# A one-hot cut into six pieces and two adds cut into halves, one such operation per unit, in a graph layer on one core

## The chip, the core and the metric

The kernel runs on one core of a Trainium2 chip. A core has five engines that run side by side and wait for each other by semaphores: TensorE (matmuls, into PSUM), VectorE, ScalarE, GpSimd and SyncE, which issues DMAs. In the profile they are called PE, DVE, ACT, POOL and SP; PEld is TensorE's loading of weights. In this kernel the DMAs that gather rows by index are issued from GpSimd, the plain ones from SyncE and, at the start and the end, ScalarE.

The metric is the device time of one execution in microseconds, lower is better. It is given as a median over several runs. The profile shows one execution.

## The reference

The layer works on 6250 nodes with 256 features and 206,250 edges (100,000 in both directions and a loop per node), sorted by destination. Cut to what matters:

```
h = relu(layernorm(x))                                   # without weights
e = relu(raw @ W_e1.T + b_e1) @ W_e2.T + b_e2            # per edge, 64 -> 256 -> 256
edge_emb = (e * (polarity + 0.01)) @ W_le.T + b_le
msg  = relu(h[src] + edge_emb)                           # a row of h gathered per edge
aggr = segment_sum(msg, dst)                             # 33 edges per node on average
t    = relu(layernorm((h + aggr) @ W_g1.T + b_g1) * ln_g + ln_b)
out  = x + t @ W_g2.T + b_g2
```

All of it is fp32.

## The kernel before

**Edges.** A tile is 128 edges, a block four tiles (512 edges), a group six blocks (3072 edges). There are 403 blocks and 68 groups, the last group of one block. Half a block, 256 edges, is called a unit; there are 806. W_e2 and W_le are multiplied into one 256x256 matrix first. The main loop runs over units u. For each it calls, in this order:

- `forward(u)`: `edge_part(u)` makes four matmuls of the unit into one PSUM buffer (line 266), of which the pool has seven, and VectorE adds a bias row and writes the result to SBUF (line 271). When u mod 4 is 1, and in the body of the run only when u mod 8 is 1, `turn_of` follows: the first layer of two pairs of blocks (line 243, 16 matmul records, eight PSUM buffers), its relu into SBUF by ScalarE (line 251) and in part VectorE (line 248), then `add_pairs`, the segment sums of finished blocks. This is called a turn below.
- `gathers(...)`: GpSimd issues the gathers of rows h[src], two per unit (line 528), tied to the last matmul of the unit. A buffer `hg` takes the rows of one unit, and there are 16.
- `whole(v)`, for a unit v that lies 22 units back at the start and one unit back at the end of the run: VectorE multiplies the edge part by the polarity, a column scalar of the tile, and adds the gathered rows (line 551, two products per unit), and ScalarE takes the relu (line 556). In the iteration of u mod 8 equal to 0 none is made in the body of the run, in the next one two.
- `due()`: one operation from a list of things that have come due. In units 0 and 1 of each eight it takes none.

**Segment sums.** `add_up` (line 566) sums a tile's messages by a matmul whose weights are a one-hot, 128 edges by 32 rows of the tile's window, one for each tile. `select(g)` makes the one-hots of a whole group in one VectorE instruction: it compares a row of 32 numbers with the rows of edges `rel`, 128 x 768 elements (line 541). It is put on the list two units after the first block of group g - 2 has been summed; three such buffers exist.

**Nodes.** The 49 windows of 128 nodes are finished as their last group is summed. `node_work(w)` puts its steps on the same list: `spread` loads x, x transposed (`hT`) and the row statistics and makes the one-hots of the window (line 629); three and four units later `ready(0)` and `ready(1)` multiply and add the statistics to `hT` (line 639, 128 x 256 each); five units later `offset` adds the last bias to x (line 205, 128 x 256). Then come `rows_of` (lines 664 and 666: sums per node, and h + aggr), `one`, `two`, `three` (the two matmuls, the layer norm, and the output).

VectorE takes its instructions in the order in which the program issues them. So in each unit its queue holds: the add of line 271, in a turn the relu of line 248, the products, and what the list gave. Line numbers are those of the kernel before.

Of the kernel before, what the change touches and what calls it, by code (L numbers as in the profile page):

```python
# [17 lines left out]
P = 128  # L18
# [33 lines left out]
def group_of(b):  # L52
    return b // L
# [40 lines left out]
def gnn_kernel(ctx: ExitStack, tc: tile.TileContext, x, src_c, dst_c, dst_r, pol_c, raw_t, w_e1t, w_e2,  # L94
# [16 lines left out]

    ident = const.tile([P, P], F32, name="ident")
    eps_t = const.tile([P, 1], F32, name="eps_t")
    we1_s = const.tile([P, D], F32, name="we1_s")
    wc_s = const.tile([P, 2, D], F32, name="wc_s")
    bc_s = const.tile([P, 2, D], F32, name="bc_s")
# [27 lines left out]
    def finish_nodes(nd, ps, w, n):  # L144

        r = w * P

        def turn(a):
            pt = ps()
            for c in range(2):  # L150
                nc.tensor.transpose(pt[:, 0, c * P:c * P + n], a[:n, c * P:(c + 1) * P], ident[:n, :n])
            aT = nd.tile([P, 2, P], F32, name="aT")
            if n == P:
                nc.scalar.activation(aT, pt[:, 0, :].rearrange("p (c n) -> p c n", c=2), AF.Copy)
            else:
                for c in range(2):
                    nc.scalar.activation(aT[:, c, :n], pt[:, 0, c * P:c * P + n], AF.Copy)
            return aT

        def first(aT, bias_by_pe=False):  # L160
            ph = ps()
            if bias_by_pe:
                nc.tensor.matmul(ph[:n, 0, :], ones[0:1, :n], bg1_b[0:1], start=True, stop=False)
            for c in range(2):
                nc.tensor.matmul(ph[:n, 0, :], aT[:, c, :n], wg1_s[:, c, :], start=c == 0 and not bias_by_pe, stop=c == 1)  # L165
            hs = nd.tile([P, D], F32, name="hs")
            if bias_by_pe:
                hb = ph[:, 0, :]
            else:
                hb = hs  # L170
                nc.vector.tensor_add(hs[:n], ph[:n, 0, :], bg1_b[:n])
            mv = row_stats(nd, n, 1, lambda i: hb[:n])
            rs = nd.tile([P, 1], F32, name="rs1")
            one_over_std(rs[:n], mv, n)
            nc.vector.tensor_scalar(hs[:n], hb[:n], mv[:n, 0, 0:1], rs[:n], op0=ALU.subtract, op1=ALU.mult)
            return hs

        def second(hs):
            pt = ps()
            for c in range(2):  # L180
                nc.tensor.transpose(pt[:, 0, c * P:c * P + n], hs[:n, c * P:(c + 1) * P], ident[:n, :n])  # L181
            nT = nd.tile([P, 2, P], F32, name="nT")
            for c in range(2):
                nc.scalar.activation(nT[:, c, :n], pt[:, 0, c * P:c * P + n], AF.Relu, bias=lnb_s[:, c:c + 1],  # L184
                                     scale=lng_s[:, c:c + 1])
            return nT

        def third(nT, xt):
            po = ps()
            for c in range(2):  # L190
                nc.tensor.matmul(po[:n, 0, :], nT[:, c, :n], wg2_s[:, c, :], start=c == 0, stop=c == 1)  # L191
            ot = nd.tile([P, D], F32, name="ot")
            nc.vector.tensor_add(ot[:n], po[:n, 0, :], xt[:n])
            for i, (a, b) in enumerate(spread_out(n)):
                eng = nc.scalar if i else nc.sync
                eng.dma_start(out=out[bass.ds(r + a, b - a), :], in_=ot[a:b])

        def load_x():
            xt = nd.tile([P, D], F32, name="xt3")
            for a, b in spread_out(n):  # L200
                nc.sync.dma_start(out=xt[a:b], in_=x[bass.ds(r + a, b - a), :])
            return xt

        def offset(xt):
            nc.vector.tensor_add(xt[:n], xt[:n], bg2_b[:n])

        return turn, first, second, third, load_x, offset

# [3 lines left out]
    with fast:  # L212
# [87 lines left out]
                turn_of(u // 4)  # L300

        nc.vector.memset(eps_t, EPS)
        nc.vector.memset(ones, 1.0)
        nc.vector.memset(rs_s, 0.0)
        nc.vector.memset(nm_s, 0.0)
# [207 lines left out]
        with tc.tile_pool(name="hg", bufs=HG) as hg_p, tc.tile_pool(name="ms", bufs=5) as ms_p, \  # L513
# [21 lines left out]

            def select(g):

                n = len(blocks_of(g)) * S
                t = g * L * S
                sel[g] = sel_p.tile([P, L * S, W], F32, name="sel")  # L540
                nc.vector.tensor_tensor(  # L541
                    sel[g][:, :n, :], iota_w.rearrange("p (o w) -> p o w", o=1).to_broadcast([P, n, W]),
                    rel[:, t:t + n].rearrange("p (t o) -> p t o", o=1).to_broadcast([P, n, W]), ALU.is_equal)

            def whole(u):

# [11 lines left out]
            def add_up(b):  # L558

                g = group_of(b)  # L560
                k = b - g * L
                if k == 0:
                    acc[g] = pd[:, g % 2, :] if g < NG - 1 else ps()[:, 0, :]
                for j in range(S):
                    m = hg[2 * b + j // 2]
                    nc.tensor.matmul(acc[g][j * W:(j + 1) * W, :], sel[g][:, k * S + j, :], m[:, j % 2, :],  # L566
                                     start=k == 0, stop=b == blocks_of(g)[-1])
                hg.pop(2 * b)
                hg.pop(2 * b + 1)
                return g if b == blocks_of(g)[-1] else None  # L570
# [16 lines left out]
            def add_pairs(last=False):  # L587

                nonlocal summed
                whole_groups = []  # L590
                while summed < NP and min(4 * summed + 4, NU) < made + last:
                    for b in (2 * summed, 2 * summed + 1):
                        if b < NB:
                            whole_groups.append(add_up(b))
                            if b % L == 0 and group_of(b) + 2 < NG:
                                at(now + 2, lambda g=group_of(b) + 2: select(g))
                    summed += 1

                for g in whole_groups:
                    keep(g)  # L600
# [2 lines left out]
            todo = {}  # L603
            now = 0
            late = {}
            ending = {-2: [], -1: []}

            def at(u, fn):
# [2 lines left out]
            def node_work(w, spread_now=False):  # L611
# [7 lines left out]
                def spread():  # L619
                    box["xt"] = load_x()  # L620
                    box["hT"] = nd.tile([P, 2, P], F32, name="hT")
                    nc.sync.dma_start(out=box["hT"][:, :, :n], in_=x_t[:, :, w * P:w * P + n])
                    st = nd.tile([P, 2, P], F32, name="stb")
                    nc.sync.dma_start(out=st, in_=st_d[w:w + 1].to_broadcast([P, 2, P]))
                    box["st"] = st
                    box["sel2"] = []
                    for g in gs:
                        s2 = sel2_p.tile([P, P], F32, name="s2")
                        nc.vector.tensor_scalar(s2, iota_p, rowid[:, g:g + 1], float(-w * P), op0=ALU.subtract,
                                                op1=ALU.is_equal)  # L630
                        box["sel2"].append(s2)
                    at(now + 3, lambda: ready(0))
                    at(now + 4, lambda: ready(1))
                    at(now + 5, lambda: offset(box["xt"]))

                def ready(i):

                    hT, st = box["hT"], box["st"]
                    nc.vector.tensor_tensor(hT[:, :, :n], hT[:, :, :n], st[:, i:i + 1, :n].to_broadcast([P, 2, n]),  # L639
                                            (ALU.mult, ALU.add)[i])  # L640

                def sums_of(part):

# [56 lines left out]

            gathers(HG)
            sums = add_pairs
            for i, fn in ((0, first_rows), (1, rows_of_edges), (3, lambda: select(0)), (5, row_numbers), (6, stats_out),
                          (7, lambda: select(1)), (8, node_weights)):
                at(LEAD + i, fn)
            for i, fn in enumerate((by_group(0, ALU.max), by_group(1, ALU.min), by_row(0, ALU.max), by_row(1, ALU.min),
                                    verdict, count, total)):
# [2 lines left out]
            for u in range(LEAD, NU):  # L710
# [8 lines left out]
                else:  # L719
                    gathers(4 * summed + HG - 4 + (u - TURN) % 4 + 1, last_z)  # L720

                while made < u + 1 - max(LEAST, LEAD - u // SHRINK) - (by_two(u // 4) and (u + 1) % 8 == TURN):
                    whole(made)
                    made += 1
                due()
                if u == NU - 24:
                    for w in range(NW):
                        if groups_of(w)[-1] == NG - 1:
                            late[w] = node_work(w, True)
                if u == LEAD + 60:  # L730
                    flag = nc.values_load(bad_i[0:1, 0:1], min_val=0, max_val=3 * P)
            while todo:
                now = min(todo)
                for fn in todo.pop(now):
                    fn()
            before, last = ending[-2], ending[-1]
            for sums_of, halves_out, rows_of, one, two, three, gs in before:
                rows_of()
# [28 lines left out]
def any_order(tc, dram, v):  # L767
# [7 lines left out]
    with tc.tile_pool(name="sc", bufs=1) as sc, tc.tile_pool(name="sk", bufs=2) as sk, \  # L775
# [78 lines left out]
        def nodes(w, n):  # L854
# [1 line left out]
            nc.sync.dma_start(out=ac[:n], in_=acc_d[bass.ds(w * P, n), :])  # L856
            turn, one, two, three, load_x, offset = v["finish_nodes"](sk, lambda: sp1.tile([P, 1, D], F32, name="ps_a"), w, n)
            xt = load_x()
            offset(xt)
            three(two(one(turn(ac))), xt)  # L860

        with tc.For_i(0, full, 1) as w:
# [65 lines left out]
```

## Time and profile before

| | |
|---|---|
| median of 3 runs | 2187.48 us (2186.34 to 2188.13) |
| profiled execution | 2189.23 us, its span 2187.4 us |
| mean granted TensorE clock | 0.997 |
| busy: TensorE, VectorE, ScalarE, GpSimd | 2169.5, 1604.4, 960.8, 1648.4 us |
| gathers, line 528 | 1612, 999 ns each in the mean |
| products, line 551 | 1612, 478 ns |
| add of the edge part, line 271 | 799, 685 ns |
| one-hot, line 541 | 68, 940 ns |
| add and multiply of h, line 639; of x, line 205 | 98, 417 ns; 49, 416 ns |

The span runs from the first to the last instruction of the program. "Busy" is time in which an engine executed an instruction, not time in which it did so at its best. A row of the groups names line, engine, operation, out<-in and shapes, then the count, the busy time, the mean length of one, and the idle time of the engine ahead of these instructions with what ended it. A row of the waits gives the total, the number of times and the longest. A row of the timeline gives the start, the length, and how many instructions were merged into it.

### The profile page before, as it was taken

Reading aid. Unit: us, or ns where it says so; the run is one execution under the profiler, and the core shown is the slowest. Engines: PE = TensorE matmul, PEld = TensorE weight load, DVE = VectorE, ACT = ScalarE, POOL = GpSimd, SP = SyncE. Lnnn points to the kernel's source line nnn. Section 1 sums busy time; section 2 is a strip of 40 time slices with the busy share of each in tenths; the row PEclk is TensorE's granted clock in tenths of the full one; section 3 lists DMA queues with packets and bytes.
Section 4 is the critical chain, followed back from the end, with each engine's and each line's share of the span. In section 5 each row is a group of like instructions: output and inputs, shape, how many; then the busy total and the mean of one; then the engine's idle time right before and its main releaser. Section 6 shows DMA issues by size and latency. Waiting matters only on the chain.

```text
span 2187.4 us, 34907 instructions
## 1 busy us (share of the span) xinstructions
PE 2169.5 (99%) x12382; PEld 1625.1 (74%) x12382; DVE 1604.4 (73%) x3470; ACT 960.8 (44%) x1701; POOL 1648.4 (75%) x1675
## 2 busy tenths in 40 slices
PE   9999999999999999999999999999999999999998
PEld 6677777777777777777677777777777777777776
DVE  7787777777777777777677777777777767777675
ACT  7444444444444444444444444343444444444443
POOL 5777777777777777777777777777777777777775
PEclk9999999999999999999999999999999999999999
DMA  9544445454545454545544445445444445454543
GB/s 313 159 134 134 138 126 157 130 149 122 151 126 155 119 155 125 151 123 151 142 122 139 142 139 151 129 121 156 139 131 128 143 130 153 131 146 130 150 123 89
DMA packets 156075, 309.17 MB, mean 141 GB/s; under 512 B 33183, under 2 KB 77944, under 8 KB 155896
## 3 DMA queue, kind: packets, MB, share of 16 engines
q0 software_dynamic: 77376, 211.39, 33.7%
q1 hardware_dynamic: 77364, 92.23, 13.7%
q10 hardware_dynamic: 1156, 3.28, 0.4%
q8 instruction: 98, 1.61, 0.3%
q14 instruction: 81, 0.66, 0.1%
HBM read 293.92 MB, written 12.85 MB: 140 GB/s over the span
## 4 chain that ended last, share of the span: by engine, by line
PE 92%; DMA 3%; POOL 2%; DVE 2%; issue 1%; ACT 1%; ACTq 0%; DVEq 0%; POOLq 0%
PE pz L266 60%; PE pz L243 16%; PE pd L566 9%; PE pz L664 3%; DMA hg<-hb_d,src_s 3%; PE pz L165 2%; PE pz L191 2%; POOL hg L528 2%; DVE msg L271 1%; PE pz L181 1%; DMA xt<-in_x_dram 0%; ACT xt L366 0%; DVE hg L551 0%; DVE st L136 0%; PE pz L307 0%
## 5 line engine op out<-in xcount | busy, mean ns | idle before, releaser
L528 POOL DMA_INDIRECT hg<-hb_d,src_s x1612 | 1611.2, 999 | 495.5 <-issue 355.3
L266 PE MATMUL pz<-wc_s,e 128*128 128x256 f32 x6448 | 1452.3, 381 | 1.3 <-ACT msg L269 1.3
L266 PEld LDWEIGHTS pz<-wc_s,e 128*128 128x128 f32 x6448 | 1208.7, 190 | 203.8 <-issue 28.8
L556 ACT ACTIVATE hg<-hg 128x512 f32<-128x512 f32 x805 | 500.5, 629 | 1048.0 <-DVE hg L551 1030.5
L551 DVE SCALAR_TENSOR_TENSOR hg<-msg,pol_s,hg 128x256 f32<-128x256 f32 x1612 | 711.3, 478 | 153.3 <-DMA hg<-hb_d,src_s 148.9
L271 DVE TENSOR_TENSOR msg<-pz,bc_s 128x512 f32<-128x512 f32 x799 | 542.9, 685 | 224.0 <-PE pz L266 223.0
L243 PE MATMUL pz<-raw,we_s 64*128 64x512 f32 x1612 | 402.8, 608 | 6.9 <-DVE msg L271 6.6
L251 ACT ACTIVATE e<-pz,vecs 128x512 f32<-128x512 f32 x605 | 361.8, 692 | 88.0 <-PE pz L243 86.9
L243 PEld LDWEIGHTS pz<-raw,we_s 64*128 64x128 f32 x1612 | 160.2, 186 | 195.6 <-issue 127.2
L248 DVE TENSOR_SCALAR e<-pz,vecs 128x512 f32<-128x512 f32 x201 | 150.5, 749 | 164.6 <-PE pz L243 164.6
L566 PE MATMUL pd<-hg,sel 128*32 128x256 f32 x3216 | 196.9, 386 | 0.0
L566 PEld LDWEIGHTS pd<-hg,sel 128*32 128x32 f32 x3216 | 95.0, 110 | 129.3 <-issue 77.6
L664 PEld LDWEIGHTS pz<-s,ms 128*128 128x128 f32 x548 | 68.7, 192 | 3.1 <-issue 0.4
L664 PE MATMUL pz<-s,ms 128*128 128x128 f32 x548 | 69.3, 275 | 0.1
L541 DVE TENSOR_TENSOR sel<-iota_w,rel 128x768 f32<-128x768 f32 x68 | 63.9, 940 | 0.0
L370 POOL TENSOR_TENSOR hb<-xt,rows_b 128x256 f32<-128x256 f32 (+1 forms) x49 | 34.1, 728 | 24.2 <-ACT xt L366 18.2
L191 PE MATMUL pz<-wg_s,nT 128*128 128x256 f32 (+1 forms) x196 | 50.6, 380 | 0.6 <-ACT nT L184 0.6
L165 PE MATMUL pz<-wg_s,hT 128*128 128x256 f32 (+1 forms) x196 | 50.5, 380 | 0.0
L577 ACT ACTIVATE ms<-pd 128x256 f32<-128x256 f32 x66 | 25.4, 384 | 51.5 <-PE pd L566 51.5
L191 PEld LDWEIGHTS pz<-wg_s,nT 128*128 128x128 f32 (+1 forms) x196 | 37.1, 190 | 5.9 <-ACT nT L184 0.8
L165 PEld LDWEIGHTS pz<-wg_s,hT 128*128 128x128 f32 (+1 forms) x196 | 37.0, 190 | 5.7 <-issue 0.3
L639 DVE TENSOR_TENSOR hT<-hT,stb 128x256 f32<-128x256 f32 x98 | 40.8, 417 | 0.0
(90 smaller groups left out, 378.2 us busy)
## 6 DMA issues: line engine op xcount, KB each, us to landing
raw<-in_raw_t_dram SPq DMA_DIRECT2D x202, 256.0 KB
hg<-hb_d,src_s POOLq DMA_INDIRECT x1612
stb<-st_d SPq DMA_DIRECT2D x49, 128.0 KB
hb_d<-hb SPq DMA_DIRECT2D x12, 512.0 KB
xt<-in_x_dram SPq DMA_DIRECT2D x48, 128.0 KB
hT<-in_x_t_dram SPq DMA_DIRECT2D x48, 128.0 KB
out_dram<-ot SPq DMA_DIRECT2D x48, 128.0 KB
xt<-in_x_dram SPq DMA_DIRECT2D x11, 512.0 KB
```

The costliest lines, as they stand in the source:

```text
L165: nc.tensor.matmul(ph[:n, 0, :], aT[:, c, :n], wg1_s[:, c, :], start=c == 0 and not bias_by_pe, stop=c == 1)
L191: nc.tensor.matmul(po[:n, 0, :], nT[:, c, :n], wg2_s[:, c, :], start=c == 0, stop=c == 1)
L243: nc.tensor.matmul(pe[s, c], we1_s[s * F:(s + 1) * F, c * P:(c + 1) * P], raw[q][s * F:(s + 1) * F, :], start=True, stop=True)
L248: nc.vector.tensor_scalar(e1[b][:, c, :], pe[s, c], be1_s[:, c:c + 1], 0.0, op0=ALU.add, op1=ALU.max)
L251: nc.scalar.activation(e1[b][:, c, :], pe[s, c], AF.Relu, bias=be1_s[:, c:c + 1])
L266: last_z = nc.tensor.matmul(pz[:, i, :], e1[b][:, c, k:k + P], wc_s[:, c, :], start=c == 0, stop=c == 1)
L271: nc.vector.tensor_add(msg[u], pz, bc_s)
L528: g = nc.gpsimd.indirect_dma_start(out=hg[u][:, i, :], out_offset=None, in_=hb_d, in_offset=bass.IndirectOffsetOnAxis(ap=src_s[:, 2 * u + ...
L551: nc.vector.scalar_tensor_tensor(hg[u][:, i, :], m[:, i, :], pol_s[:, 2 * u + i:2 * u + i + 1], hg[u][:, i, :], op0=ALU.mult, op1=ALU.add)
L556: nc.scalar.activation(hg[u], hg[u], AF.Relu)
L566: nc.tensor.matmul(acc[g][j * W:(j + 1) * W, :], sel[g][:, k * S + j, :], m[:, j % 2, :], start=k == 0, stop=b == blocks_of(g)[-1])
L664: nc.tensor.matmul(pa[:, c, :n], ms[g][:, c * P:(c + 1) * P], box["sel2"][i][:, :n], start=i == 0, stop=i == len(gs) - 1)
```

## The change

`select` no longer issues its instruction. It returns one entry per block of the group, and these are put into a queue `rest`; each entry makes the one-hots of one block's four tiles, 128 x 128 elements. `ready` and `offset` work on one half of 128 columns per call, and their four and two calls are put into a queue `steps`, due three units after `spread`. In each unit `piece()` takes one entry: from `steps` if its first is due, else from `rest`. It is called behind `forward` and `gathers` and ahead of `whole`. When more than six entries are in `rest`, a second one is taken behind `due`. `add_up` takes out what is still left for its group.

All three operations become a `scalar_tensor_tensor` whose scalar is a column of zeros, `zero_c`: (tensor + 0) op tensor. They were `tensor_tensor`. The values computed are the same.

```diff
+    zero_c = const.tile([P, 1], F32, name="zero_c")
...
-        def offset(xt):
-            nc.vector.tensor_add(xt[:n], xt[:n], bg2_b[:n])
+        def offset(xt, c):
+            h = slice(c * P, (c + 1) * P)
+            nc.vector.scalar_tensor_tensor(xt[:n, h], xt[:n, h], zero_c[:n], bg2_b[:n, h], op0=ALU.add, op1=ALU.add)
...
+        nc.vector.memset(zero_c, 0.0)
...
             def select(g):
-                n = len(blocks_of(g)) * S
-                t = g * L * S
-                sel[g] = sel_p.tile([P, L * S, W], F32, name="sel")
-                nc.vector.tensor_tensor(
-                    sel[g][:, :n, :], iota_w.rearrange("p (o w) -> p o w", o=1).to_broadcast([P, n, W]),
-                    rel[:, t:t + n].rearrange("p (t o) -> p t o", o=1).to_broadcast([P, n, W]), ALU.is_equal)
+                return [(g, lambda k=k: rows_of_block(g, k)) for k in range(len(blocks_of(g)))]
+
+            def rows_of_block(g, k):
+                t = (g * L + k) * S
+                if k == 0:
+                    sel[g] = sel_p.tile([P, L * S, W], F32, name="sel")
+                nc.vector.scalar_tensor_tensor(
+                    sel[g][:, k * S:(k + 1) * S, :], iota_w.rearrange("p (o w) -> p o w", o=1).to_broadcast([P, S, W]),
+                    zero_c, rel[:, t:t + S].rearrange("p (t o) -> p t o", o=1).to_broadcast([P, S, W]), op0=ALU.add,
+                    op1=ALU.is_equal)
+
+            def piece():
+                if steps and steps[0][0] <= now:
+                    steps.popleft()[1]()
+                elif rest:
+                    rest.popleft()[1]()
...
                 if k == 0:
                     acc[g] = pd[:, g % 2, :] if g < NG - 1 else ps()[:, 0, :]
+                    while rest and rest[0][0] <= g:
+                        rest.popleft()[1]()
...
                             if b % L == 0 and group_of(b) + 2 < NG:
-                                at(now + 2, lambda g=group_of(b) + 2: select(g))
+                                rest.extend(select(group_of(b) + 2))
...
-                    at(now + 3, lambda: ready(0))
-                    at(now + 4, lambda: ready(1))
-                    at(now + 5, lambda: offset(box["xt"]))
+                    steps.extend((now + 3, lambda i=i, c=c: ready(i, c)) for i in range(2) for c in range(2))
+                    steps.extend((now + 3, lambda c=c: offset(box["xt"], c)) for c in range(2))

-                def ready(i):
+                def ready(i, c):
                     hT, st = box["hT"], box["st"]
-                    nc.vector.tensor_tensor(hT[:, :, :n], hT[:, :, :n], st[:, i:i + 1, :n].to_broadcast([P, 2, n]),
-                                            (ALU.mult, ALU.add)[i])
+                    nc.vector.scalar_tensor_tensor(hT[:, c, :n], hT[:, c, :n], zero_c, st[:, i, :n], op0=ALU.add,
+                                                   op1=(ALU.mult, ALU.add)[i])
...
-            for i, fn in (..., (3, lambda: select(0)), ..., (7, lambda: select(1)), (8, node_weights)):
+            for i, fn in (..., (3, lambda: rest.extend(select(0) + select(1))), ..., (8, node_weights)):
                 at(LEAD + i, fn)
...
+                piece()
                 while made < u + 1 - max(LEAST, LEAD - u // SHRINK) - (by_two(u // 4) and (u + 1) % 8 == TURN):
                     whole(made)
                     made += 1
                 due()
+                if len(rest) > 6:
+                    piece()
...
+            while steps:
+                steps.popleft()[1]()
```

The path `any_order`, taken only for inputs in another order, calls `offset` for both halves; it isn't run here.

## The prediction

> **What bounds the kernel now.** I read the head of the page first, then the groups by line, then the waits, and last the timeline around single gathers. By the head TensorE is busy for 99% of the span and GpSimd for 75%:
>
> ```profile
> span 2187.4 us, 34907 instructions
> PE 2169.5 (99%) x12382; PEld 1625.1 (74%) x12382; DVE 1604.4 (73%) x3470; ACT 960.8 (44%) x1701; POOL 1648.4 (75%) x1675
> ```
>
> That 75% misleads. The gathers of line 528 have these rows in the groups, in the view of their line (shortest/median/longest, first and last start) and in the waits (total, times, longest):
>
> ```profile
> L528 POOL DMA_INDIRECT hg<-hb_d,src_s x1612 | 1611.2, 999 | 495.5 <-issue 355.3
> ...
> L528 POOL DMA_INDIRECT hg<-hb_d,src_s x1612: 940/947/2088, 64.5 to 2168.0; - x180
> ...
> POOL hg L528 <- PE pz L266: 39.6, 130, 0.3
> POOL hg L528 <- ACT hg L556: 26.5, 87, 0.3
> ```
>
> The reader is to see that busy and idle add up: 1611.2 + 495.5 is, but for 2.3 ahead of the first, the whole stretch from 64.5 us to the end of the last at 2168.9, and the idle is 495.5 / 1612 = 0.31 us ahead of each gather, no longer after a wait for TensorE or ScalarE than without one. GpSimd goes from gather to gather without being starved once. Its time is 1612 x (0.947 + 0.305) = 2018 us plus what the gathers take over their median, 1612 x (999 - 947) = 84 us.
>
> TensorE pays for the lateness in the first layer's turns:
>
> ```profile
> L243 PE MATMUL pz<-raw,we_s 64*128 64x512 f32 x1612 | 402.8, 608 | 6.9 <-DVE msg L271 6.6
> ...
> 1190.54 3.70 PE L243 MATMUL pz<-raw,we_s 64*128 64x512 f32 x16
> ...
> 1014.55 4.83 PE L243 MATMUL pz<-raw,we_s 64*128 64x512 f32 x16
> ...
> 1017.40 0.29 PEld L243 LDWEIGHTS pz<-raw,we_s 64*128 64x128 f32 x2 [0.84 <-DVE msg L271]
> ...
> DVE hg L551 <- DMA hg<-hb_d,src_s: 148.9, 199, 2.8
> ```
>
> A clean turn takes 3.70 us for 16 records, the one at 1014.55 takes 4.83 because a PSUM buffer still waits for VectorE's add. VectorE is late since its products wait for gathered rows (148.9 us). Over all turns 402.8 - 1612/16 x 3.70 = 30 us are lost, with the 6.9 idle 37 us. TensorE could thus end at about 2187.4 - 37 = 2150, GpSimd without its excess 84 us earlier than now. GpSimd is the bound, and TensorE stands 37 us behind it.
>
> **Where the 84 us come from.** The timeline puts it on VectorE instructions with two SBUF tensors:
>
> ```profile
> 1012.03 0.48 DVE L551 SCALAR_TENSOR_TENSOR hg<-msg,pol_s,hg 128x256 f32<-128x256 f32 x1 [1.08 <-DMA hg<-hb_d,src_s]
> 1012.14 1.20 POOL L528 DMA_INDIRECT hg<-hb_d,src_s  x1 [0.30 <-DMA hg<-hb_d,src_s]
> ...
> 78.02 1.66 DVE L551 SCALAR_TENSOR_TENSOR hg<-msg,pol_s,hg 128x256 f32<-128x256 f32 x4
> 78.12 1.19 POOL L528 DMA_INDIRECT hg<-hb_d,src_s  x1 [0.30 <-issue]
> ...
> 2161.34 0.87 DVE L551 SCALAR_TENSOR_TENSOR hg<-msg,pol_s,hg 128x256 f32<-128x256 f32 x2
> 2161.52 1.12 POOL L528 DMA_INDIRECT hg<-hb_d,src_s  x1 [0.30 <-issue]
> ...
> 151.74 1.31 POOL L528 DMA_INDIRECT hg<-hb_d,src_s  x1 [0.30 <-issue]
> 151.81 0.42 DVE L205 TENSOR_TENSOR xt<-xt,rows_b 128x256 f32<-128x256 f32 x1
> ...
> 2124.01 1.38 POOL L528 DMA_INDIRECT hg<-hb_d,src_s  x1 [0.30 <-issue]
> 2124.20 0.37 DVE L639 TENSOR_TENSOR hT<-hT,stb 128x212 f32<-128x212 f32 x1
> ...
> 81.71 0.95 DVE L541 TENSOR_TENSOR sel<-iota_w,rel 128x768 f32<-128x768 f32 x1
> 82.11 1.37 POOL L528 DMA_INDIRECT hg<-hb_d,src_s  x1 [0.30 <-issue]
> ...
> 2166.45 0.42 DVE L639 TENSOR_TENSOR hT<-hT,stb 128x256 f32<-128x256 f32 x1
> 2166.68 1.00 POOL L528 DMA_INDIRECT hg<-hb_d,src_s  x1 [0.30 <-issue]
> ```
>
> In the first pair the product ends at 1012.51 and the gather at 1013.34, 0.83 us later; at 82.11 it is again 0.82 us after the one-hot's end. So a gather needs something 0.947 - 0.82 = 0.13 us after its start, and while such an instruction runs it stands. Three cases follow from the rows. A product behind a product lets a gather in: at 2161.52 it ends (2162.64) 0.82 us after the first product's end (2161.82), though the second began at 2161.73; so at 78.12, in a row of four. That is so in all 251 such meetings that I count, these two being the last and the first. An add of line 205, 639 or 541 right behind a product often doesn't: at 151.74 and 2124.01 the gather began before the add and still ended 0.82 us after the add's end. I count 45 such gathers in the timeline (the two shown are the first and the last), 26 us of excess. 66 more began their need inside one of these adds (82.11 and 2166.68 are first and last), 19 us. The other 39 us lie on products alone. The product has a column scalar, these adds have none.
>
> **The change part by part.** Durations of VectorE:
>
> ```profile
> L551 DVE SCALAR_TENSOR_TENSOR hg<-msg,pol_s,hg 128x256 f32<-128x256 f32 x1612 | 711.3, 478 | 153.3 <-DMA hg<-hb_d,src_s 148.9
> L541 DVE TENSOR_TENSOR sel<-iota_w,rel 128x768 f32<-128x768 f32 x67 | 63.7, 950 | 0.0
> L541 DVE TENSOR_TENSOR sel<-iota_w,rel 128x128 f32<-128x128 f32 x1 | 0.3, 283 | 0.0
> L639 DVE TENSOR_TENSOR hT<-hT,stb 128x256 f32<-128x256 f32 x96 | 40.1, 417 | 0.0
> L205 DVE TENSOR_TENSOR xt<-xt,rows_b 128x256 f32<-128x256 f32 x48 | 20.0, 416 | 0.0
> L271 DVE TENSOR_TENSOR msg<-pz,bc_s 128x512 f32<-128x512 f32 x799 | 542.9, 685 | 224.0 <-PE pz L266 223.0
> ```
>
> *The new pieces.* No row shows a two-tensor instruction with a column at 128 elements. The plain add at 128 takes 283 ns (lower end). The product takes 478 at 256 elements, 61 more than an add of that size (417), and an element costs (950 - 417) / 512 = 1.04 ns: 478 - 133 = 345, the value I take, as it is the same operation; 478 is the upper end. Two products take 0.87 us, so the second starts 0.39 after the first: 0.085 overlap, and a piece takes 0.26 of VectorE's queue.
>
> *VectorE's sum.* 67 x 6 + 1 = 403 pieces of one-hot at 0.26 replace 67 at 0.865: 104.8 - 58 = +47 us. 196 halves of h replace 98 adds at 0.335: +18. 98 halves of x replace 49: +9. Together +74 us on 1604 (with the ends of the price +32 and +168). None of it stands on the path by itself: VectorE idles 224 us ahead of line 271, waiting for TensorE. It is 0.76 us more per turn of eight units (98 turns), and that cover is gone in turns where the products wait for rows; there, work ahead of the wait costs nothing, work behind it makes line 271 later.
> The VectorE page of the Trainium skill (VectorE: DVE Perf Modes, section on the TRN2 errata) says a SBUF instruction pays a fixed latency each time and advises tiles of 512 elements or more, which speaks against cutting 768 into six; its formula (N + 151) / 0.96 would make a piece 291 ns, an estimate near the lower end. The trace agrees that the fixed part is most of a small one (283 ns at 128, 950 at 768).
>
> *GpSimd's sum.* Gone: the 19 us of the 66 direct gathers, and of the 26 us all but the rest of the product that the gather met anyway (45 x about 0.15 = 6). New: 403 + 196 + 98 = 697 pieces of 0.345 us that hold a gather. If gathers (one per 2104/1612 = 1.31 us) met them freely, 697 x 0.345²/2 / 1.31 = 32 us. Products by that formula would cost 1612 x 0.478²/2 / 1.31 = 141 us, and they cost 39 + 6: about a third, which would make it 10 us. The old adds by it: (67 x 0.95² + 147 x 0.417²)/2 / 1.31 = 33, and they cost 39. I take 20, between the ends 10 and 40. New excess 39 + 6 + 20 = 65 instead of 84: -19 us (bounds -29 and +1).
>
> *Place and order.* The operation now stands behind line 271's add, which reads PSUM, and ahead of the products, whose column lets a gather in. It delays two products by 0.26 us per unit, ScalarE's relu waits for those, and behind them the segment sums and the buffers that the gathers need; the gathers' queue is late anyway. The old list skipped units 0 and 1 of each eight, ahead of the first layer's turn; the new call doesn't, so up to 0.52 us more stands close before that turn. I cost this at 3 us of the saving. The halves of h still come three units after their loads are issued, but ahead of the products: if a load were late, products and adds would queue behind it; line 639 shows 0.0 idle now, so nothing. One-hot is asked for two groups ahead as before, six pieces in some 12 units; the forced flush should find nothing. Shorter lists for the other node steps, one memset: nothing measurable. No DMA is added or moved.
>
> Sum: -19 + 3 = -16 us. The profiled execution took 2189.2 us (span 2187.4), 1.7 above the median 2187.5; so 2173 profiled, 2171 for the median.
>
> **The rivals.** *Both bounds free (faster still).* Pieces meet few gathers (10 us) and GpSimd saves 29 us, still inside the 37 that TensorE can give: 2187.5 - 29 = 2158. For it: the third that products show. Against it: a turn then has no reserve.
> *The pieces hold as the adds did.* If the column lets nobody in, meetings cost 32 to 40 us beside the old 39: the change does nothing, 2187 ± 4. Against it: no product behind a product was waited through in 251 meetings (78.12 to 2161.52).
> The page on SBUF (SBUF — State Buffer, Who interferes with whom) in the Trainium skill states that an instruction with two SBUF inputs holds the pair shared with GpSimd for its whole length, whatever its scalar is; by that rule this rival is right. The trace agrees on the hold itself and shows the gap behind products, of which the page says nothing.
> *Slower: VectorE becomes late at the turns.* The added 0.76 us per turn falls behind the last awaited rows, and line 271's add misses its time: the pool has seven PSUM buffers, a matmul of the turn takes 3.70 / 8 = 0.46 us, so the seventh needs the buffer of the unit just made 2.8 us after the turn's start, and the add takes 0.69. From some 2 us of lateness each further us costs TensorE one. At 0.76 in half of 98 turns it costs 37 us, less the 19 saved by GpSimd: +18, 2205. For it: 1014.55 shows turns that are at this point now, and the two quiet units lose their quiet. Against it: the 224 us of waiting for TensorE at line 271, 2.3 us a turn.
>
> **How the numbers follow.** Forecast 0.54, both bounds free 0.12, nothing 0.13, slower 0.21. The predicted time is 2171 us. Its own range is 2160 to 2181; with the rivals 2157 to 2202. A measurement of this kernel can't tell less than 0.2% (4.4 us) from no change. Faster 0.66, same 0.13, slower 0.21.
>
> **What would show it.** Right: line 528's mean falls from 999 to about 987 ns with idle still 0.31 us each and the last start near 2152; no gather of 1.9 us; line 243's busy time falls by some 15 us; the pieces take about 345 ns, VectorE's busy time rises by some 70. Wrong: a mean of 528 that stays at 999 (the pieces hold), or gathers with idle over 0.31 us and more than 402.8 us in line 243 (VectorE late).

## The result and the profile after

The changed kernel takes 2171.57 us in the median (2171.04 to 2173.39, 6 runs), the kernel before 2187.41 (2186.11 to 2189.05, 6 runs): a ratio of 0.993, 95% interval 0.9917 to 0.9942. The profiled execution is shorter by the same 17.9 us as its span, 2169.5 instead of 2187.4. The prediction said 2171.

The head of the page after, its groups (line, engine, operation, out<-in, count, then busy us, mean ns, idle us ahead and its releasers), and from the view of the gathers' line the shortest, median and longest one with the first and last start:

```profile
span 2169.5 us, 35373 instructions
PE 2155.0 (99%) x12382; PEld 1616.9 (75%) x12382; DVE 1677.7 (77%) x3953; ACT 964.0 (44%) x1701; POOL 1619.4 (75%) x1675
...
L531 POOL DMA_INDIRECT hg<-hb_d,src_s x1612 | 1582.1, 981 | 505.7 <-issue 358.5
L566 DVE SCALAR_TENSOR_TENSOR hg<-msg,pol_s,hg 128x256 f32<-128x256 f32 x1612 | 699.1, 478 | 38.6 <-DMA hg<-hb_d,src_s 37.7
L245 PE MATMUL pz<-raw,we_s 64*128 64x512 f32 x1612 | 389.7, 607 | 4.4 <-DVE msg L273 4.0
L548 DVE SCALAR_TENSOR_TENSOR sel<-iota_w,zero_c,rel 128x128 f32<-128x128 f32 x403 | 137.8, 342 | 2.3 <-PE pd L583 2.3
...
L531 POOL DMA_INDIRECT hg<-hb_d,src_s x1612: 942/949/2235, 63.3 to 2148.0; - x180
```

The reader is to see four things. VectorE is busy for 73 us more, and the kernel is faster all the same. The mean gather fell from 999 to 981 ns, 1612 x 18 = 29 us on GpSimd. VectorE's products wait 38 us for gathered rows instead of 149. And TensorE is busy in the first layer (line 245, formerly 243) for 13 us less, with 2.5 us less idle ahead of it. The last gather starts 20 us earlier, at 2148.0.

One number went the other way: GpSimd's idle time ahead of gathers rose from 495.5 to 505.7 us. The waits (total, times, longest) say where; the first two rows are of before, the others of after. Before, the longest behind a matmul of the first layer was 0.3 us, the fixed gap, and now it is 1.7. In the timeline 20 gathers stand idle for more than 0.4 us, before the change 6.

```profile
POOL hg L528 <- ACT e L251: 21.6, 68, 1.1
POOL hg L528 <- PE pz L243: 20.7, 68, 0.3
...
POOL hg L531 <- issue: 358.5, 1151, 2.0
...
POOL hg L531 <- PE pz L245: 21.9, 67, 1.7
```

Two gathers that met a piece, from the timeline after (start us, us):

```profile
2128.67 0.34 DVE L548 SCALAR_TENSOR_TENSOR sel<-iota_w,zero_c,rel 128x128 f32<-128x128 f32 x1
2128.81 1.02 POOL L531 DMA_INDIRECT hg<-hb_d,src_s  x1 [0.31 <-ACT hg L571]
2128.93 0.88 DVE L566 SCALAR_TENSOR_TENSOR hg<-msg,pol_s,hg 128x256 f32<-128x256 f32 x2
...
109.22 0.94 POOL L531 DMA_INDIRECT hg<-hb_d,src_s  x1 [0.30 <-issue]
109.34 0.33 DVE L548 SCALAR_TENSOR_TENSOR sel<-iota_w,zero_c,rel 128x128 f32<-128x128 f32 x1
```

The gather at 2128.81 ends at 2129.83, 0.82 us after the piece (2129.01) and not after the products that follow it. The one at 109.22 started 0.12 us before its piece and wasn't held at all: 0.94 us is less than the median. These are the last and the first of 100 gathers that met a one-hot piece with products behind it; none was carried into the products, and they cost 4.4 us together.

### The profile page after: what moved, and what is told of

Same layout as the page of the kernel before. It is cut to its first block, busy times and chain, and to the rows that moved or that the text cites. A ratio compares the mean times of both kernels' runs of the same rounds, so it can differ in the third digit from the quotient of the medians.

```text
span 2169.5 us, 35373 instructions
## 1 busy us (share of the span) xinstructions
PE 2155.0 (99%) x12382; PEld 1616.9 (75%) x12382; DVE 1677.7 (77%) x3953; ACT 964.0 (44%) x1701; POOL 1619.4 (75%) x1675
## 4 chain that ended last, share of the span: by engine, by line
PE 92%; DMA 1%; POOL 1%; DVE 1%; issue 1%; ACT 0%; SPq 0%; POOLq 0%; DVEq 0%; ACTq 0%
PE pz L268 60%; PE pz L245 16%; PE pd L583 9%; PE pz L682 3%; PE pz L192 2%; PE pz L166 2%; DMA hg<-hb_d,src_s 1%; POOL hg L531 1%; PE pz L182 1%; DVE hg L566 0%; DVE msg L273 0%; DMA hb_d<-hb 0%; ACT e L253 0%; DVE st L137 0%; PE pz L666 0%
## 5 line engine op out<-in xcount | busy, mean ns | idle before, releaser
L531 POOL DMA_INDIRECT hg<-hb_d,src_s x1612 | 1582.1, 981 | 505.7 <-issue 358.5
L566 DVE SCALAR_TENSOR_TENSOR hg<-msg,pol_s,hg 128x256 f32<-128x256 f32 x1612 | 699.1, 478 | 38.6 <-DMA hg<-hb_d,src_s 37.7
L245 PE MATMUL pz<-raw,we_s 64*128 64x512 f32 x1612 | 389.7, 607 | 4.4 <-DVE msg L273 4.0
L245 PEld LDWEIGHTS pz<-raw,we_s 64*128 64x128 f32 x1612 | 152.4, 187 | 187.9 <-issue 137.3
L548 DVE SCALAR_TENSOR_TENSOR sel<-iota_w,zero_c,rel 128x128 f32<-128x128 f32 x403 | 137.8, 342 | 2.3 <-PE pd L583 2.3
L657 DVE SCALAR_TENSOR_TENSOR hT<-hT,zero_c,stb 128x128 f32<-128x128 f32 (+1 forms) x196 | 67.0, 342 | 0.9 <-DMA stb<-st_d 0.9
```

The costliest lines, as they stand in the source:

```text
L245: nc.tensor.matmul(pe[s, c], we1_s[s * F:(s + 1) * F, c * P:(c + 1) * P], raw[q][s * F:(s + 1) * F, :], start=True, stop=True)
L531: g = nc.gpsimd.indirect_dma_start(out=hg[u][:, i, :], out_offset=None, in_=hb_d, in_offset=bass.IndirectOffsetOnAxis(ap=src_s[:, 2 * u + ...
L548: nc.vector.scalar_tensor_tensor(sel[g][:, k * S:(k + 1) * S, :], iota_w.rearrange("p (o w) -> p o w", o=1).to_broadcast([P, S, W]), zero_ ...
L566: nc.vector.scalar_tensor_tensor(hg[u][:, i, :], m[:, i, :], pol_s[:, 2 * u + i:2 * u + i + 1], hg[u][:, i, :], op0=ALU.mult, op1=ALU.add)
```

## The experiments

The theory: GpSimd is the bound; its gathers are held while a VectorE instruction with two SBUF tensors runs, and are carried through two of them in a row when the second has no column. The rivals: only the cutting counts; only the place counts; the added VectorE load is what the time pays for.

A program's runs were spread over several chips. Seven of the twelve fell on chips where the records grant TensorE a clock of 0.94 to 0.96 and every kernel, that of before too, takes 2550 to 2622 us in the median; they stand by themselves at the end of this section. The other five ran at 0.995 or more, and the verdicts rest on those.

**The column alone.** The kernel before, its three adds at their old sizes and places:

```diff
-                nc.vector.tensor_tensor(sel[g][:, :n, :], iota..., rel..., ALU.is_equal)
+                nc.vector.scalar_tensor_tensor(sel[g][:, :n, :], iota..., zero_c, rel..., op0=ALU.add, op1=ALU.is_equal)
```

and likewise for h and x.

> The column alone, old sizes and places, on a chip with full clock. On the chip that held TensorE back no gather was carried through there (0 of 60 meetings). Theory: excess 64 us instead of 84, 2172 to 2177 us. Rival (size and place are what counts): 2185 to 2190 us.

Measured: 2174.15 us against 2186.46, ratio 0.9945 (0.9931 to 0.9958). Its groups:

```profile
L530 POOL DMA_INDIRECT hg<-hb_d,src_s x1612 | 1595.9, 990 | 496.7 <-issue 353.9
L543 DVE SCALAR_TENSOR_TENSOR sel<-iota_w,zero_c,rel 128x768 f32<-128x768 f32 x68 | 68.0, 1001 | 0.0
```

The excess is 1612 x (990 - 947) = 69 us instead of 84, where 64 was expected. VectorE works longer (the one-hot 1001 ns instead of 940), and the kernel gains 12 us. In the timeline none of the 70 gathers that met a product with one of these adds behind it was carried through, where 45 of 87 were before. The column works without any cutting or moving.

**Place and cutting, without the column.** The changed kernel with its pieces as plain `tensor_tensor`:

> The plain pieces at the new place once more, on a chip that grants TensorE its full clock. Theory (nothing can be carried through behind an add that reads PSUM): excess about 53 us, GpSimd the bound; 2168 to 2172 us. Rival (the column itself frees the gathers): excess about 75 us, 2182 us or more.

Measured: 2169.23 against 2186.23, ratio 0.9921 (0.9905 to 0.9936), which can't be told from the changed kernel's 0.993.

```profile
L531 POOL DMA_INDIRECT hg<-hb_d,src_s x1612 | 1573.1, 976 | 510.6 <-issue 359.1
L548 DVE TENSOR_TENSOR sel<-iota_w,rel 128x128 f32<-128x128 f32 x403 | 114.1, 283 | 2.4 <-PE pd L582 2.3
```

The excess is 47 us, the least of all. Ahead of the products, behind an add that reads PSUM, the column isn't needed, and it costs 59 ns a piece. (The adds uncut at this place were not run at full clock.)

**Cutting alone.** The same plain pieces, called behind the products:

```diff
-                piece()
                 while made < ...:
                     whole(made)
                     made += 1
+                piece()
                 due()
```

> Plain pieces behind the products, on a chip with full clock. Theory: over half of the gathers that meet a product ahead of such a piece are carried through (117 of 176 on the other chip); excess 85 to 100 us, GpSimd the bound again; 2185 to 2200 us, so cutting and spreading alone are worth nothing. Rival (short pieces hold little): 2170 to 2174 us.

Measured: 2186.61 against 2186.46, ratio 1.0002 (0.9993 to 1.0011): nothing. The excess is 1612 x (992 - 947) = 73 us, less than expected and 11 less than before; half of that is lost again as waiting (table below), and the profiled execution of before was itself 1.7 us above its median. The timeline shows what a piece without a column does here, and when:

```profile
L531 POOL DMA_INDIRECT hg<-hb_d,src_s x1612 | 1599.8, 992 | 501.0 <-issue 358.1 <-PE pz L268 36.2 <-ACT hg L570 24.7
...
173.63 0.28 DVE L207 TENSOR_TENSOR xt<-xt,rows_b 128x128 f32<-128x128 f32 x1
173.83 0.68 DVE L273 TENSOR_TENSOR msg<-pz,bc_s 128x512 f32<-128x512 f32 x1
174.43 0.87 DVE L565 SCALAR_TENSOR_TENSOR hg<-msg,pol_s,hg 128x256 f32<-128x256 f32 x2
175.04 1.28 POOL L531 DMA_INDIRECT hg<-hb_d,src_s  x1 [0.30 <-issue]
175.22 0.28 DVE L548 TENSOR_TENSOR sel<-iota_w,rel 128x128 f32<-128x128 f32 x1
...
167.18 0.69 DVE L273 TENSOR_TENSOR msg<-pz,bc_s 128x512 f32<-128x512 f32 x1 [1.07 <-PE pz L268]
167.79 0.87 DVE L565 SCALAR_TENSOR_TENSOR hg<-msg,pol_s,hg 128x256 f32<-128x256 f32 x2
168.28 1.20 POOL L531 DMA_INDIRECT hg<-hb_d,src_s  x1 [0.30 <-issue]
168.58 0.28 DVE L656 TENSOR_TENSOR hT<-hT,stb 128x128 f32<-128x128 f32 x1
```

At 175.04 the gather ends at 176.32, 0.82 us after the piece's end (175.50): carried through. At 168.28 it ends at 169.48, 0.82 us after the second product's end (168.66), though the piece began at 168.58. The difference is the idle time in brackets: VectorE had waited for TensorE just ahead of line 273's add. Of all 218 gathers that met a product with a piece behind it, 70 were carried through. Counting those with just this add and two products ahead of the piece: where VectorE had waited ahead of the add, 0 of 95 meetings were carried through, and where it had run on without a pause from the piece before, 46 of 55. In the kernel before it was 0 of 16 and 36 of 52. So a gather is carried through, by these counts, where VectorE is behind.

**Column and cutting, old place.** The changed kernel with `piece()` moved as above:

> Pieces with the column behind the products, on a chip with full clock. Theory: none carried through, but a gather let in behind a product meets the piece or the other product more often than in the changed kernel; excess 60 to 70 us; 2172 to 2180 us. Rival (the place is what counts, the column does nothing): as tt_behind, 2185 us or more.

Measured: 2173.28 against 2186.46, ratio 0.9946 (0.9932 to 0.9959).

```profile
L531 POOL DMA_INDIRECT hg<-hb_d,src_s x1612 | 1578.6, 979 | 506.7 <-issue 368.6 <-PE pz L268 31.1 <-ACT e L253 29.4
```

The excess of 52 us is below the range expected, and again nothing was carried through: 0 of 189 meetings, in 75 of them with VectorE running on without a pause as above. The column at the old place and the plain pieces at the new one each do the work; together they add little.

**Every piece twice.** A second, unused one-hot piece behind each piece:

```diff
                 if steps and steps[0][0] <= now:
                     steps.popleft()[1]()
+                    idle()
                 elif rest:
                     rest.popleft()[1]()
+                    idle()
```

> The changed kernel with a second, unused 128-element piece issued behind every piece: VectorE gets some 690 x 0.26 = 180 us more, ahead of the products. Theory (VectorE has room, GpSimd is the bound): the extra pieces hold gathers for 8 us or so; 2172 to 2185 us. Rival (the added load makes VectorE late at the turns): line 245 loses 40 us or more, 2200 us or more.

Measured: 2220.14 against 2186.46, ratio 1.0154 (1.014 to 1.0168), 49 us above the changed kernel. By time and by line 246 the rival's numbers came out. But it isn't TensorE's turns that set the time:

```profile
L532 POOL DMA_INDIRECT hg<-hb_d,src_s x1612 | 1631.8, 1012 | 505.2 <-issue 355.6
L246 PE MATMUL pz<-raw,we_s 64*128 64x512 f32 x1612 | 423.4, 615 | 18.4 <-DVE msg L274 18.0
...
2155.81 0.34 DVE L556 SCALAR_TENSOR_TENSOR spare_s<-iota_w,zero_c,rel 128x128 f32<-128x128 f32 x1
2156.07 0.87 DVE L576 SCALAR_TENSOR_TENSOR hg<-msg,pol_s,hg 128x256 f32<-128x256 f32 x2
2156.15 1.62 POOL L532 DMA_INDIRECT hg<-hb_d,src_s  x1 [0.30 <-issue]
```

GpSimd's idle time is that of the changed kernel (505 us), so it didn't wait more for the others; its gathers take 1612 x (1012 - 981) = 50 us longer, which is the whole loss. And the gather at 2156.15 ends at 2157.77, 0.83 us after the end of the second product (2156.94): with two pieces ahead, products carry gathers through although they have a column, in 68 of 302 meetings of a product followed by a product. These meetings cost 68 us where they cost 22 in the changed kernel, which is nearly all of the 50. Where VectorE had idled within the four instructions ahead of the products none of 158 was carried through, otherwise 68 of 144. So the theory's bound held and its rule fell: the column is no guarantee when VectorE is far behind.

**The bound, over all of them.** Excess is 1612 x (mean - 947 ns), added idle is GpSimd's idle ahead of gathers over the fixed 1612 x 0.305 = 492 us; both from the rows shown, in us:

| kernel | excess | added idle | span | span less both |
|---|---|---|---|---|
| before | 84 | 4 | 2187.4 | 2099 |
| pieces plain, behind | 73 | 9 | 2184.8 | 2103 |
| column alone | 69 | 5 | 2174.4 | 2100 |
| changed kernel | 55 | 14 | 2169.5 | 2101 |
| column, behind | 52 | 15 | 2170.3 | 2103 |
| pieces plain, ahead | 47 | 19 | 2167.5 | 2102 |
| every piece twice | 105 | 14 | 2219.1 | 2101 |

The last column proves nothing by itself: it is what is left of a chain of 1612 gathers when excess and added idle are taken out, and on the chips below, where GpSimd isn't the bound, it comes to 2110 to 2114. What shows the bound is the added idle: in all seven kernels GpSimd waited for others for only 4 to 19 us (373 to 443 on the chips below), while its excess moves by 58 us and the span by 52. The reserve is small, and what is saved in held gathers is given back in part as waiting, of which the rows name TensorE and ScalarE: from 69 to 47 us of excess only 7 us of the 22 are left in the span.

**On chips that hold TensorE back.** Here GpSimd idles for 860 to 935 us, so it isn't the bound. The granted clock is some 5% lower in the records and the time of the kernel before 17 to 19% longer; what makes the rest isn't shown. The same four kernels, and three more: a second instruction per piece that reads one SBUF tensor only, the adds uncut and plain but in the new place, and the changed kernel without pieces in units 0 and 1 of each eight:

```diff
+                nc.vector.tensor_scalar(spare_s, wc_s[:, 0, :192], zero_c, 0.0, op0=ALU.subtract, op1=ALU.is_equal)   # twice_free
...
-                return [(g, lambda k=k: rows_of_block(g, k)) for k in range(len(blocks_of(g)))]
+                return [(g, lambda: rows_of_group(g))]                                     # whole_ahead
...
-                piece()
+                if not (by_two(u // 4) and u % 8 in QUIET):                                # quiet
+                    piece()
```

> The kernel before, with the three adds at their old sizes and places, but given the column of zeros. Theory (a column lets a gather in behind a product): the gathers that were carried through a product into the add vanish, excess of the gathers from 84 us to about 64; the 66 direct meetings stay; VectorE pays 214 x 0.061 = 13 us more; 2174 us. Rival (only the size and the place of the pieces count): nothing gained, 2187 to 2190 us.

> The changed kernel, its pieces at the same size and place, but as plain adds without a column (283 ns instead of 342). Theory: ahead of a piece now stands the add of the edge part, which reads PSUM, so nothing can be carried through; excess about 53 us as against 55.5 in the changed kernel, VectorE 40 us less busy; 2168 to 2172 us. Rival (the column itself is what frees the gathers, wherever the piece stands): excess about 75 us, 2182 us or more.

> The changed kernel, its pieces with the column, but put behind the products instead of ahead of them. Theory: the column lets gathers in behind a product as well; excess 55 to 62 us; 2170 to 2175 us. Rival (the place is what counts): 2180 us or more.

> The pieces as plain adds and behind the products. Theory: of the gathers that meet a product with such an add behind it about half are carried through, as before the change (45 of 87), now some 200 meetings, 100 times 0.2 us; excess about 75 us; 2179 to 2184 us, the slowest of the four with pieces or the column. Rival (only the size counts, short pieces hold little): as the changed kernel, 2170 to 2173 us.

> As the doubled pieces, but the second instruction behind each piece reads one SBUF tensor and a column (192 elements, about the same 0.26 us of VectorE's queue) and should hold no gather. Theory (what the doubled pieces cost, 48 us, was held gathers and not VectorE's load): excess about 55 us as in the changed kernel, 2172 to 2182 us. Rival (VectorE is late at the turns by the load): line 245 at 415 us or more, 2205 to 2220 us.

> The adds uncut and without a column, 768 and 256 elements, but in the new place ahead of the products. Theory: nothing is carried through; the one-hot met directly still holds (about 50 meetings of 0.33 us), excess 57 to 65 us, 2170 to 2176 us, so the cutting is worth some 3 us. Rival (the cutting is what counts): 2183 to 2188 us.

> The changed kernel, but no piece in units 0 and 1 of each eight, ahead of the first layer's turns; what is left over goes into the second call behind the products. If the lost quiet costs the 3 us of the prediction: 2167 to 2170 us and line 245 below 386 us. If it costs nothing: 2170 to 2174 us.

Measured against the kernel before on the same chip (2592.05 us for the first four, 2550.01 for the last three), ratio and interval: column alone 1.0022 (1.0004 to 1.004), pieces plain ahead 1.0129 (1.0099 to 1.0159), column behind 1.0099 (1.0068 to 1.0129), pieces plain behind 1.0009 (0.9986 to 1.0032), twice_free 1.0204 (1.0177 to 1.0231), whole_ahead 1.0077 (1.0049 to 1.0104), quiet 1.0081 (1.0057 to 1.0106). The rows of the plain pieces ahead there, head and gathers:

```profile
PE 2392.8 (92%) x12382; PEld 1675.7 (64%) x12382; DVE 1622.0 (62%) x3953; ACT 964.4 (37%) x1701; POOL 1620.4 (62%) x1675
...
PEclk9899999999999999999999998999999999999999
...
L531 POOL DMA_INDIRECT hg<-hb_d,src_s x1612 | 1583.1, 982 | 934.8 <-issue 676.8 <-ACT e L253 88.9 <-ACT ms L593 68.4
```

The gathers take 982 ns, nearly as at full clock (976), and it helps nothing, because 935 us of idle stand between them. No time of the expectations can be judged by these runs. Their timelines still count meetings: the column alone 0 of 60 carried through, the plain pieces behind 117 of 176. In whole_ahead the plain one-hot of 768 elements carried nobody through, but the 45 gathers that met it were held for 26 us, where 111 meetings with its plain 128-element pieces ahead cost 6 us on such a chip and 89 cost 5 us at full clock. That is what the cutting is worth in the new place, in held time. In twice_free the added instructions held some 1 us themselves, and yet 26 of 346 product pairs carried a gather through. Why these kernels are slower there, by up to 1.3% without twice_free, wasn't settled; the changed kernel itself wasn't run there. Whether the doubled load costs anything without held gathers, and what the quiet units are worth, stays open at full clock.

## Why the prediction was right, step by step

*The bound.* Right: GpSimd goes from gather to gather, and in seven kernels it waits for others for no more than 19 us of a span near 2200. One reading was too strong: gathers did wait before the change too, five of them behind the first for 0.14 to 0.82 us over the fixed gap, 2.3 us together (the row of line 251 above has one of 1.1).

*The piece's price.* 345 ns taken, 342 measured (283 plain, the lower end, in the plain kernel). The estimate of 291 by the formula of the Trainium skill's page VectorE: DVE Perf Modes (section on the TRN2 errata) is near the plain one; the formula has no term for the column. *VectorE's sum.* +74 us forecast, 1604.4 to 1677.7 = +73 measured, and none of it showed in the time by itself.

*GpSimd's sum.* The direction was right and a term was mis-sized. The pieces were put at 20 us of held gathers between the ends 10 and 40; in the timeline after, 185 gathers met a piece and lost 7.7 us together, below the lower end. Their number is what free arrival gives, 697 x 0.345 / 1.31 = 184. What the formula had wrong is the hold: it lets a piece hold a gather from the piece's start. But of the 54 gathers that started before the piece or up to 0.03 us after it, one was held; the border lies some 0.07 us after the start (last section). With the 0.13 us from a gather's start to its need, needs in the first 0.2 us of a piece are mostly free, and 697 x 0.145² / 2 / 1.31 = 6 us, an estimate from these counts, is near the 7.7. For products the same gives 1612 x 0.278² / 2 / 1.31 = 48 us, near the prediction's 45, which is the third of 141 that it found; of a shorter instruction less than a third is left. The products' term itself was right: 43 us after, 39 + 6 forecast. So the excess came down to 55 us, not 65, and GpSimd saved 29 instead of 19.

*Place and order.* The 3 us held back here were too small, and for another reason than the quiet units, which no run at full clock isolates. What went missing is 10 us of new idle time on GpSimd: once its backlog is gone at places, it waits for TensorE's and ScalarE's releases. 29 - 10 and 1 from the first gather, at 63.3 instead of 64.5, make the 20 us at the last gather; 17.9 are left at the end. The forecast of 16 stands on a saving 10 too small and a loss 7 too small. The errors nearly cancel, and that the time came out within 1 us is luck; the direction and the bound are not. The rival "both bounds free" had GpSimd's saving right (29) and was wrong that it passes through.

*The range.* It doesn't follow from its terms at the upper end: with GpSimd's +1 and the 3 of place and order the sum is 2187.5 + 4 = 2191, while the range ends at 2181; and the slower rival's 2205 lies above the 2202 given with the rivals.

*The pieces hold as the adds did.* Fell for this kernel: none of the 100 gathers at a one-hot piece was carried on. But its opposite, as I put it (the column lets gathers in), isn't a rule either: with the piece ahead of the products the column does nothing that the place doesn't do, and behind a late VectorE it fails. By the page SBUF — State Buffer of the Trainium skill (SBUF: two separate sides) a VectorE instruction with two SBUF inputs and a GpSimd one that reads SBUF share a lock, and whichever starts first has it for the whole instruction; it makes no exception for a scalar. The trace agrees with it in each single hold (0.82 us from the holder's end to the gather's) and in the gathers that start first, which beside products and pieces with the column weren't held (1 of 761, last section). It differs where of 1072 gathers that started up to 0.1 us later only 379 were held, and it doesn't show that a gather holds VectorE in turn: products that started behind it took 0.48 us like the others. The page says nothing of the step from one instruction to the next, and there the column alone was worth 12 us, so the measurement decides.

*VectorE late at the turns.* Didn't happen: line 245 lost less time, not more. The doubled pieces show that the slower side is near, and that it comes over held gathers.

*What would show it.* Line 528's mean at 987 ns: 981. Idle still 0.31 us each: 0.314, with single waits up to 2 us, which I hadn't expected. Last start near 2152: 2148. No gather of 1.9 us: none but one at the start (2235 ns at 71.7 us, behind a subtraction over 1608 elements, line 459), where before there were ten more between 1.9 and 2.0.

## What to carry to other kernels

An engine with a fixed gap ahead of every instruction and no longer one is the bound, whatever its busy share says: add busy and idle over the stretch, and look for instructions longer than their median. When such an engine is held by another one's instructions, look first at what stands ahead of these: cut and behind something that doesn't hold it (here an add from PSUM) they gained 17 us, rewritten with a column at their old place 12, and cut alone nothing. What the move alone is worth wasn't measured at full clock. Expect the saving to pass through only until the next engine's lead is used up.

## What the runs showed that was not expected

Whether a VectorE instruction with two SBUF tensors holds a gather goes by which of the two starts first. This is counted in the seven traces at full clock, over gathers whose need (0.13 us after the start) falls inside the instruction, more than 0.025 us ahead of its end, and that weren't carried through; held means over 0.012 us longer than 0.947. Beside products and pieces with the column, 1 of 761 gathers that started before the instruction was held, 379 of 1072 that started up to 0.1 us after it, and all 1839 that started later. Beside plain adds it was 7 of 67 that started before and 202 of 208 that started after. So the first part of each instruction holds nobody, and with the column that part is some 0.07 us longer (an estimate from these counts), about what the column adds to the length (342 ns instead of 283).

A gather was carried through two VectorE instructions in a row where VectorE had been running without a pause: 0 of 95 against 46 of 55 in the plain pieces behind the products, 0 of 16 against 36 of 52 before the change. A column scalar makes it rarer but doesn't exclude it: 0 of 251 product pairs before the change, 2 of 265 after, 68 of 302 with two pieces ahead. The later border of a column would leave a gather that one instruction lets go a little more time ahead of the next; that is a guess which no run isolates, and it doesn't explain the 68.

A VectorE instruction that nobody needs cost 49 us through another engine's instructions being 31 ns longer in the mean, while VectorE itself still had 17% of the span free (busy 1843.9 of 2219.1 us).
